# Loop one of a two-block network: where lower parts, weight copies and weight pieces stand in a step

## The chip, the core and the metric

The kernel runs on one core of a Trainium2 chip. The core has TensorE (PE in the profile; PEld is its weight loading), VectorE (DVE), ScalarE (ACT), GpSimd (POOL) and SyncE (SP), each with a queue of its own that is worked off in order, and 16 DMA engines. Matmuls read SBUF and write PSUM, which is used here as eight banks of 128 x 512 float32. The metric is the device time of one execution in microseconds (us), the median of several runs. Times inside an execution come from one profiled execution and are counted from the start of its span.

## What is computed

Two blocks over x of 32 batches, 128 rows, 512 columns, each steered by a condition of 512 numbers per batch. The first block's attention has 16 heads of 32 columns; loop one computes this block:

```python
h = _sln(hidden, w, ln_g, ln_b, Wg, bg, Wb, bb)
qkv = (h @ Wqkv.T + bqkv).reshape(B, N, num_heads, hd, 3)
...
energy = jnp.einsum('bhqd,bhkd->bhqk', q, k)
att = jax.nn.softmax(energy, axis=-1) / D ** 0.5
out = jnp.einsum('bhqk,bhkd->bhqd', att, v)
out = jnp.moveaxis(out, 1, 2).reshape(B, N, D)
out = out @ Wp.T + bp
h1 = out + hidden
h2 = _sln(h1, w, ln_g, ln_b, Wg, bg, Wb, bb)
return h2 + h1
```

`_sln` is a layer norm whose scale and shift come from the condition. The second block takes this result: an RMS norm with scale and shift, attention with one head of 512 columns, a projection, and an MLP of 512 to 2048 to 512 with an exact gelu, each with its residual. All tensors are float32.

## The kernel before

**Precision.** A float32 product is made from three products of reduced float32 parts: every operand is split into an upper part (a rounding copy, `h` at the end of a tile's name) and a lower part (operand minus upper part, `l`), and `mm3` sums upper x upper, lower x upper and upper x lower in one PSUM bank. So every operand costs a copy, mostly on ACT, and a subtraction on DVE or POOL before its matmuls can start.

**Tiling.** A batch is one tile of 128 x 512. Four batches make a group (G = 4) and 512 columns are four chunks of 128 (KC = 4). Eight groups times four chunks make the 32 steps of loop one (STEPS): step s belongs to group s // 4 and chunk s % 4, and handles in one go the four heads of this chunk for the four batches of the group. The rest of the program, about 545 us to the end, is block two, and is not touched by the change.

**One step.** The order of the calls in the loop's body is the order of each engine's queue; the compiler only adds semaphores and picks the buffers of a pool (the next free one of its kind). A step s issues, in this order:

- `energies(s+1)`: 16 matmuls of q and k into four banks (`pse`), four reduces on DVE (L577) to the negative maxima `nm`, a cast and a subtraction (L578, L579).
- `scores0(s)`: the energies again, transposed, on top of the spread maxima of the step before (`pst`, L602 and L606), in two banks of the kind `mm`, which `psv` and `psp` use too, and two of the kind `s`.
- `turned.low` (L461): the lower part of the normed batch whose upper part was made in the step before.
- `heads_out(s-1)`: attention times values (`pso`, L629) and the sums of the exponentials (`pss`, L634), in banks that `pse` used; their reciprocal by a logarithm and an exponential on ACT (L639, L640). `exponentials(s)` on ACT (L616).
- `past.first`, `past.sums`: the second layer norm's statistics of the batch that was finished in the step before.
- `divided0(s-1)`: three DVE instructions (L647 to L649) divide the heads' outputs; then ACT makes the upper part (`hi`, L651) and POOL the lower part (`lo`, L652). At the first step of a group it stands ahead of `end.bias` and `end.more`, otherwise behind them.
- `qk0(s+2)`: 12 matmuls for q (`psq`) and 12 for k (`psk`) of a coming step, from the normed batches of its group; ACT writes both with their bias (L548). Its second argument orders them by part instead of by chunk at the start of a group.
- between the two: `maxima(s+1)` (a transpose) and `spread_maxima(s+1)` (DVE, L590).
- `end.stream`: 12 matmuls (`psp`) for one batch of the group whose attention was done four steps ago, from `o`'s upper and lower parts; `end.bias` (POOL, L668) and `end.add` (DVE, L683) add bias, residual and product.
- `past.second` (L702), then `ready.merge` (DVE, L431: brings a batch that the DMA has transposed into the order of the matmuls) and `ready.rest` (ACT: four L448 with scale and shift, and the upper part, L457).
- `new.stats`, `end.add`, `new.norm`, and `past.third` (L711).
- work of single steps: `extras`, among them `weighted` in steps 0 and 1 (DVE, L505 and L507: four instructions whose result a matmul in the next step reads), and `split_w` in steps 0 to 3 (ACT L145, POOL L146).
- `values0`: 12 matmuls for v (`psv`), copied by ACT (L532).
- `new.halves`: ACT splits a normed batch into 16-bit halves (L422), and SP's queue starts its DMA transpose.
- from step 4 to 23, `weights.heads` and `weights.tails`: parts of the MLP's first weights are copied to upper parts by ACT (L920) and lower parts by POOL (L927), and SP's queue writes both out to DRAM (`put`). Per weight piece of five steps the numbers of copies are 2, 1, 1, 2, 1.

In the last three steps the loop also multiplies two weights of block two (`l1_vp`, `psvp`): four chunks `w1c2_0` to `w1c2_3` are loaded into buffers that q and k tiles use too, and each product is split by ACT (L126) and DVE (L127). `psvp0` takes a bank of the kind `s`. `vp_at` says that chunk 0 is requested in step 29, both 1 and 2 in step 30, and chunk 3 in step 31; the requests come a step ahead of the products.

Of the kernel before, what the change touches and what calls it, by code (L numbers as in the profile page):

```python
# [9 lines left out]
FP = mybir.dt.float32  # L10
# [3 lines left out]
ALU = mybir.AluOpType  # L14
# [4 lines left out]
KC = D // P  # L19
# [22 lines left out]
def cond_seq_kernel(ctx: ExitStack, tc, x, condT, wcond, w0, w1, wk1, wm1, wm2, cols, rows, out):  # L42
# [600 lines left out]
    def divided0(s):  # L643

        g, c = divmod(s, KC)
        pso, pss, w = es.pop(s)
        nc.vector.tensor_tensor(pss, pss, w, ALU.mult)  # L647
        nc.vector.tensor_tensor(w, pso, w, ALU.mult)
        nc.vector.scalar_tensor_tensor(w, pss, 2.0, w, ALU.subtract, ALU.mult, reverse0=True)  # L649
        hi, lo = (t[:, c] for t in os_[g])  # L650
        nc.scalar.copy(hi, w)  # L651
        nc.gpsimd.tensor_tensor(lo, w, hi.bitcast(FP), ALU.subtract)  # L652

    class End:

# [541 lines left out]
    with tc.manual_schedule(engines=ordered):  # L1197
# [88 lines left out]
        def l1_chunk(j, c):  # L1286
            return load(d_tile(f"w1c{j}_{c}", FP, (P, KC, P)), w1[:, j, :, ts(c, P)])
# [6 lines left out]
        def stage(work, get):  # L1294
            def begin():
                got = get()
                return lambda: work(got)

            return begin
# [10 lines left out]
            27: stage(l1_row, lambda: (weighted("wrow1", L1[3], C_BV1), row_of(R_BP1))),  # L1310
        }

        def vp_stage(c):
            return stage(lambda a: l1_vp(a, L1[3], c, s_tile if c == 0 else e_bank), lambda: l1_chunk(2, c))

        vp_at = {STEPS - 3: (0,), STEPS - 2: (1, 2), STEPS - 1: (3,)}
        FIRST1 = STEPS - G - 2

        def coming(s):
# [5 lines left out]
        CQ = range(7, 15, 2)  # L1325
        W_FIRST, W_STEPS = 4, len(Weights.TURNS)
        ready, new, end, past = new, coming(0), None, None
        staged = turned = None
        vps = []
        for s in range(STEPS):  # L1330
            last = s == STEPS - 1
            vps, vps_next = vps, [vp_stage(c) for c in vp_at.get(s + 1, ())]
            end = End(s - G, True, nc.scalar) if s >= G else None
            if not last:
                energies(s + 1)
            scores0(s)
            if turned:
                turned.low(nc.vector)
                turned = None
            if s:  # L1340
                heads_out(s - 1)
            exponentials(s)
            if past:
                past.first()
                past.sums()
            if s and s % KC == 0:
                divided0(s - 1)
            if end:
                end.bias()
                end.more()  # L1350
            if s % KC:
                divided0(s - 1)
            if staged:
                staged()
            if s > STEPS - 3:
                vps.pop(0)()
            vps_next = [begin() for begin in vps_next]
            q, k = qk0(s + 2, (s + 2) % KC == 0) if s + 2 < STEPS else ([], [])
            run(q)
            if not last:  # L1360
                maxima(s + 1)
                spread_maxima(s + 1)
            run(k)
            if end:
                run(end.stream())
            if s > STEPS - 3:
                end.add()
            if past:
                past.second()
            if ready and not last:  # L1370
                ready.merge()
                ready.rest()
            if new:
                new.stats()
            if end and s <= STEPS - 3:
                end.add()
            if new:
                new.norm()
            if s == KC + 1:
                cond_features()  # L1380
            if past:
                past.third()
            if "cq" in L1:
                L1.pop("cq")()
            if s < KC:
                split_w(W0["p"], raw["p"], s, nc.gpsimd)
            staged = extras[s + 1]() if s + 1 in extras else None
            if s <= B - G:
                run(values0(s - 1 + G))
            if vps:  # L1390
                vps.pop(0)()
            if new:
                new.halves()
            coming_new = None if last else coming(s + 1)
            q2, late = divmod(s - W_FIRST, 3)
            if not late and 0 <= q2 < 4:
                nc.scalar.dma_start(out=w2d[q2], in_=wm2[:, q2])
            wn, wj = divmod(s - W_FIRST, W_STEPS)
            if 0 <= wn < KC:
                weights.heads(wj)  # L1400
                weights.tails(wj)
            if not last:
                turned, ready, new = ready, new, coming_new
            vps = vps_next
            past = end
            if s in CQ:
                L1["cq"] = l1_cq(CQ.index(s))
            if s == 2:
                later["mods"] = r_tile("mods")
            wn, wj = divmod(s + 1 - W_FIRST, W_STEPS)  # L1410
            if 0 <= wn < KC and wj == 0:
                weights = Weights(wn)
            if s == STEPS - 2:
                l1_load()
        heads_out(STEPS - 1)
        past.first()
        past.sums()
        divided0(STEPS - 1)
        K = keys1(0)
        run(K[0])  # L1420

# [187 lines left out]
```

## Time and profile before

| | us |
|---|---|
| median of 3 runs (1446.51, 1448.55, 1450.84) | 1448.55 |
| the profiled execution's own time | 1445.18 |
| its span | 1443.0 |
| loop one within the span | 33.9 to 544.9 |
| TensorE busy | 1428.2 |
| VectorE busy | 1036.4 |
| ScalarE busy | 756.3 |
| GpSimd busy | 432.8 |
| mean granted TensorE clock | 0.999 |

The profiled execution is 2.2 us longer than its span and 3.4 us shorter than the median of the runs. In the span a group of lines of the profile reads: line and engine, what is written and read, how often, the time busy, the mean of one in nanoseconds, and the idle time of the engine ahead of it with the instruction that ended most of it. The chain of waits, followed back from the last instruction, goes along TensorE for 90% of the span:

```profile
PE 90%; DVE 6%; ACT 2%; DMA 2%; POOL 0%; issue 0%; SPq 0%; ACTq 0%; POOLq 0%; DVEq 0%
```

These are groups of the page that belong to loop one or reach into it:

```profile
L431 DVE COPY tn<-tn 128x1024 uint16<-128x1024 uint16 x90 | 103.9, 1155 | 5.3 <-DMA tn<-tn 5.3
...
L577 DVE TENSOR_REDUCE nm<-pse 128x4 f32<-128x512 f32 x128 | 79.5, 683 | 32.2 <-PE pse L565 31.9
...
L616 ACT ACTIVATE e<-pst 128x512 f32<-128x512 f32 x128 | 65.3, 595 | 1.3 <-PE pst L606 1.3
...
L448 ACT ACTIVATE tn<-tn,mod 128x128 f32<-128x128 f32 x104 | 42.9, 483 | 30.9 <-DVE tn L431 30.9
...
L927 POOL TENSOR_TENSOR wml<-wm,wmh 128x512 fp32r<-128x512 f32 x28 | 35.4, 1277 | 69.0 <-ACT wmh L920 64.8
...
L668 POOL TENSOR_TENSOR xe<-xe,row 128x512 f32<-128x512 f32 x32 | 44.9, 1403 | 6.7 <-DMA xe<-in_x 6.7
```

### The profile page before, as it was taken

How to read it: one execution, taken by the hardware profiler on the slowest of the kernel's cores; microseconds unless marked ns; L12 is line 12 of the kernel's file. 1: busy time of each engine (PE TensorE's matmuls, PEld its weight loads, DVE VectorE, ACT ScalarE, POOL GpSimd, SP SyncE). 2: the span in 40 equal slices, each digit the busy share in tenths (PEclk: the TensorE clock that was granted, in tenths of full speed). 3: DMA queues.
4: the chain of work that ended last, by engine and by line, in shares of the span. 5: the costliest groups of instructions: out<-in, count | busy, mean ns of one | idle time of the engine just before them, and what ended most of it. 6: DMA issues, size and time to landing. Idle time of an engine off the chain costs nothing.

```text
span 1443.0 us, 24819 instructions
## 1 busy us (share of the span) xinstructions
PE 1428.2 (99%) x9224; PEld 1146.3 (79%) x9224; DVE 1036.4 (72%) x1909; ACT 756.3 (52%) x1392; POOL 432.8 (30%) x393
## 2 busy tenths in 40 slices
PE   9999999999999999999999999999999999999998
PEld 5777777777777758888888888888888888888887
DVE  6778989898997878899987766655566556753442
ACT  4566565566664545677776444535453544523231
POOL 0124645555553334556550324000030002210000
PEclk9999999999999999999999999999999999999999
DMA  8267777967664555778888867747684777834450
GB/s 311 75 192 192 205 209 199 249 158 196 174 166 143 132 187 165 200 210 222 205 215 321 293 213 227 272 157 227 207 309 134 218 230 213 290 124 169 159 182 31
DMA packets 227873, 287.82 MB, mean 199 GB/s; under 512 B 107396, under 2 KB 138244, under 8 KB 226216
## 3 DMA queue, kind: packets, MB, share of 16 engines
q1 hardware_dynamic: 209888, 211.68, 50.0%
q10 hardware_dynamic: 17864, 74.55, 15.7%
q8 instruction: 73, 1.20, 0.3%
q14 instruction: 48, 0.39, 0.1%
HBM read 193.18 MB, written 73.60 MB: 185 GB/s over the span
## 4 chain that ended last, share of the span: by engine, by line
PE 90%; DVE 6%; ACT 2%; DMA 2%; POOL 0%; issue 0%; SPq 0%; ACTq 0%; POOLq 0%; DVEq 0%
PE acc L1053 24%; PE psh L164 21%; PE psp L164 6%; PE psq L164 5%; PE psV L164 5%; PE psT L164 5%; PE psk L164 5%; PE psv L164 5%; PE pse L565 2%; PE pso L629 2%; PE pss L818 2%; DVE nm L577 1%; PE pss L634 1%; PE pst L606 1%; PE pso L164 1%; PE psvp L757 1%
## 5 line engine op out<-in xcount | busy, mean ns | idle before, releaser
L337 POOL TENSOR_TENSOR rn<-vn,neghalf 128x1 f32<-128x1 f32 x96 | 58.1, 605 | 468.7 <-DVE vn L335 355.8
L422 ACT COPY tn<-x 128x1024 uint16<-128x1024 uint16 x90 | 94.1, 1047 | 52.4 <-DVE x L408 51.8
L991 ACT ACTIVATE c<-c,col 128x512 f32<-128x512 f32 x64 | 46.4, 725 | 141.9 <-DVE c L1016 88.8
L431 DVE COPY tn<-tn 128x1024 uint16<-128x1024 uint16 x90 | 103.9, 1155 | 5.3 <-DMA tn<-tn 5.3
L1069 POOL TENSOR_TENSOR xe<-xe,row 128x512 f32<-128x512 f32 x32 | 45.9, 1467 | 200.7 <-DVE u_7s L1045 116.4
L577 DVE TENSOR_REDUCE nm<-pse 128x4 f32<-128x512 f32 x128 | 79.5, 683 | 32.2 <-PE pse L565 31.9
L1006 DVE TENSOR_TENSOR c<-psh,ca 128x512 f32<-128x512 f32 x32 | 22.1, 692 | 87.5 <-PE psh L164 86.2
L616 ACT ACTIVATE e<-pst 128x512 f32<-128x512 f32 x128 | 65.3, 595 | 1.3 <-PE pst L606 1.3
L325 DVE BATCH_NORM_STATS2 stn<-x 128x6 f32<-128x512 f32 x96 | 65.2, 679 | 0.0
L408 DVE TENSOR_SCALAR x<-x,rn 128x512 f32<-128x512 f32 x64 | 58.3, 911 | 8.3 <-POOL rn L337 7.5
L337 POOL TENSOR_TENSOR re<-ve,neghalf 128x1 f32<-128x1 f32 x32 | 30.9, 965 | 105.6 <-DVE ve L330 102.0
L448 ACT ACTIVATE tn<-tn,mod 128x128 f32<-128x128 f32 x104 | 42.9, 483 | 30.9 <-DVE tn L431 30.9
L448 ACT ACTIVATE tn<-tn,mods 128x128 f32<-128x128 f32 x128 | 52.6, 484 | 11.7 <-DVE tn L431 11.7
L639 ACT ACTIVATE rs<-pss 128x512 f32<-128x512 f32 x32 | 19.1, 597 | 72.9 <-PE pss L634 72.9
L927 POOL TENSOR_TENSOR wml<-wm,wmh 128x512 fp32r<-128x512 f32 x28 | 35.4, 1277 | 69.0 <-ACT wmh L920 64.8
L1019 DVE TENSOR_TENSOR ca<-psh,ca 128x512 f32<-128x512 f32 x32 | 22.1, 691 | 41.8 <-PE psh L164 41.8
L668 POOL TENSOR_TENSOR xe<-xe,row 128x512 f32<-128x512 f32 x32 | 44.9, 1403 | 6.7 <-DMA xe<-in_x 6.7
L991 ACT ACTIVATE cb<-cb,col 128x512 f32<-128x512 f32 x32 | 23.2, 725 | 41.0 <-DVE cb L1020 41.0
L1073 DVE TENSOR_TENSOR xe<-acc,xe 128x512 f32<-128x512 f32 x32 | 21.1, 688 | 32.0 <-PE acc L1053 32.0
L565 PEld LDWEIGHTS pse<-qk 32*128 32x128 f32 x1024 | 32.1, 186 | 13.6 <-issue 5.3
L1003 ACT COPY ca<-psh 128x512 f32<-128x512 f32 x32 | 18.4, 575 | 43.0 <-PE psh L164 41.9
L565 PE MATMUL pse<-qk 32*128 32x128 f32 x1024 | 38.6, 283 | 1.5 <-ACT qk L548 1.4
(1387 smaller groups left out, 4702.7 us busy)
## 6 DMA issues: line engine op xcount, KB each, us to landing
mod<-mod SPq DMA_DIRECT2D x32, 512.0 KB, 4.6
ur<-ud SPq DMA_DIRECT2D x64, 256.0 KB, 4.4
xs<-xe SPq DMA_DIRECT2D x60, 256.0 KB, 2.8
xe<-xs SPq DMA_DIRECT2D x60, 256.0 KB, 3.0
x<-xs SPq DMA_DIRECT2D x59, 256.0 KB, 3.8
scw<-scw SPq DMA_DIRECT2D x32, 256.0 KB, 4.2
hTd<-tn SPq DMA_DIRECT2D x32, 256.0 KB, 6.6
hT<-hTd SPq DMA_DIRECT2D x32, 256.0 KB, 4.7
```

The costliest lines, as they stand in the source:

```text
L164: nc.tensor.matmul(st["ps"], *calls[j], start=(j == 0), stop=(j == n - 1))
L325: nc.vector.bn_stats(st, t)
L337: nc.gpsimd.tensor_tensor(r, v, neghalf, ALU.pow)
L408: nc.vector.tensor_scalar(X, X, r, None, ALU.mult)
L422: nc.scalar.copy(halves.rearrange("p (e d) -> p e d", e=2), X.bitcast(U16).rearrange("p (d e) -> p e d", e=2),)
L431: nc.vector.tensor_copy(self.a.bitcast(U16).rearrange("p (f e) -> p e f", e=2), self.t.bitcast(U16).rearrange("p (e f) -> p e f", e=2),)
L448: nc.scalar.activation(dst[:, c], self.a[:, ts(c, P)], AF.Identity, bias=m[:, q + B : q + B + 1], scale=m[:, q : q + 1],)
L565: nc.tensor.matmul(banks[r][:, ts(i, P)], q[32 * r : 32 * r + 32, ts(i, P)], k[32 * r : 32 * r + 32, ts(i, P)], start=True, stop=True,)
L577: nc.vector.tensor_reduce(nm[:, r], chunks(banks[r]), AX.X, ALU.max, negate=True)
L616: nc.scalar.activation(e, es[s][r], AF.Exp)
L991: nc.scalar.activation(t[nm], t[nm], AF.Gelu, bias=col[:, C_B1 + f : C_B1 + f + 1], scale=1.0)
L1053: nc.tensor.matmul(accs[i], u[pa][:, ts(i, P)], wb[f // 4][pb][:, f % 4, :], start=(first and j == 0), stop=(last and j == len(PARTS) - 1),)
```

## The change

Only the body of loop one and `divided0` change; the arithmetic stays as it is.

- The subtraction that makes the lower part of the heads' outputs leaves POOL (L652). A new function `lower0` issues it on DVE, behind `spread_maxima` and ahead of `past.second`. The upper copy on ACT stays in `divided0`.
- A batch's lower part (L461) is issued at the end of the step that makes its upper part, behind `past.third`, and no longer in the next step behind the reduces. It stands ahead of the `weighted` instructions of the step's extras.
- `weights.heads` and `weights.tails` move from the end of a step to a place ahead of `past.third`, and so ahead of the copy of v and of `new.halves` with its transpose.
- `divided0` stands behind `end.bias` and `end.more` in every step, and `qk0` orders its 12 matmuls by chunk in every step.
- The chunks for `l1_vp` are requested one at a time: chunk 0 in step 29 behind the k matmuls, chunk 1 at the end of step 29, chunk 2 in step 30 ahead of `past.first`, chunk 3 in step 30 behind the k matmuls. The products keep their places: 0 at the end of step 29, 1 in the middle and 2 at the end of step 30, 3 in the middle of step 31.

```diff
@@ -647,9 +647,14 @@
         nc.vector.tensor_tensor(pss, pss, w, ALU.mult)
         nc.vector.tensor_tensor(w, pso, w, ALU.mult)
         nc.vector.scalar_tensor_tensor(w, pss, 2.0, w, ALU.subtract, ALU.mult, reverse0=True)
+        nc.scalar.copy(os_[g][0][:, c], w)
+        es[s] = w
+
+    def lower0(s):
+
+        g, c = divmod(s, KC)
         hi, lo = (t[:, c] for t in os_[g])
-        nc.scalar.copy(hi, w)
-        nc.gpsimd.tensor_tensor(lo, w, hi.bitcast(FP), ALU.subtract)
+        nc.vector.tensor_tensor(lo, es.pop(s), hi.bitcast(FP), ALU.subtract)
 
     class End:
 
@@ -1310,10 +1315,14 @@
             27: stage(l1_row, lambda: (weighted("wrow1", L1[3], C_BV1), row_of(R_BP1))),
         }
 
-        def vp_stage(c):
-            return stage(lambda a: l1_vp(a, L1[3], c, s_tile if c == 0 else e_bank), lambda: l1_chunk(2, c))
-
-        vp_at = {STEPS - 3: (0,), STEPS - 2: (1, 2), STEPS - 1: (3,)}
+        chunk = {}
+
+        def vp_load(c):
+            chunk[c] = l1_chunk(2, c)
+
+        def vp(c):
+            l1_vp(chunk.pop(c), L1[3], c, e_bank if c else s_tile)
+
         FIRST1 = STEPS - G - 2
 
         def coming(s):
@@ -1325,42 +1334,40 @@
         CQ = range(7, 15, 2)
         W_FIRST, W_STEPS = 4, len(Weights.TURNS)
         ready, new, end, past = new, coming(0), None, None
-        staged = turned = None
-        vps = []
+        staged = None
         for s in range(STEPS):
             last = s == STEPS - 1
-            vps, vps_next = vps, [vp_stage(c) for c in vp_at.get(s + 1, ())]
             end = End(s - G, True, nc.scalar) if s >= G else None
             if not last:
                 energies(s + 1)
             scores0(s)
-            if turned:
-                turned.low(nc.vector)
-                turned = None
             if s:
                 heads_out(s - 1)
             exponentials(s)
+            if s == STEPS - 2:
+                vp_load(2)
             if past:
                 past.first()
                 past.sums()
-            if s and s % KC == 0:
-                divided0(s - 1)
             if end:
                 end.bias()
                 end.more()
-            if s % KC:
+            if s:
                 divided0(s - 1)
             if staged:
                 staged()
             if s > STEPS - 3:
-                vps.pop(0)()
-            vps_next = [begin() for begin in vps_next]
-            q, k = qk0(s + 2, (s + 2) % KC == 0) if s + 2 < STEPS else ([], [])
+                vp(1 if s == STEPS - 2 else 3)
+            q, k = qk0(s + 2) if s + 2 < STEPS else ([], [])
             run(q)
             if not last:
                 maxima(s + 1)
                 spread_maxima(s + 1)
+            if s:
+                lower0(s - 1)
             run(k)
+            if s > STEPS - 4 and not last:
+                vp_load(0 if s == STEPS - 3 else 3)
             if end:
                 run(end.stream())
             if s > STEPS - 3:
@@ -1378,8 +1385,14 @@
                 new.norm()
             if s == KC + 1:
                 cond_features()
+            wn, wj = divmod(s - W_FIRST, W_STEPS)
+            if 0 <= wn < KC:
+                weights.heads(wj)
+                weights.tails(wj)
             if past:
                 past.third()
+            if ready and not last:
+                ready.low(nc.vector)
             if "cq" in L1:
                 L1.pop("cq")()
             if s < KC:
@@ -1387,21 +1400,18 @@
             staged = extras[s + 1]() if s + 1 in extras else None
             if s <= B - G:
                 run(values0(s - 1 + G))
-            if vps:
-                vps.pop(0)()
+            if STEPS - 4 < s < STEPS - 1:
+                vp(0 if s == STEPS - 3 else 2)
             if new:
                 new.halves()
+            if s == STEPS - 3:
+                vp_load(1)
             coming_new = None if last else coming(s + 1)
             q2, late = divmod(s - W_FIRST, 3)
             if not late and 0 <= q2 < 4:
                 nc.scalar.dma_start(out=w2d[q2], in_=wm2[:, q2])
-            wn, wj = divmod(s - W_FIRST, W_STEPS)
-            if 0 <= wn < KC:
-                weights.heads(wj)
-                weights.tails(wj)
             if not last:
-                turned, ready, new = ready, new, coming_new
-            vps = vps_next
+                ready, new = new, coming_new
             past = end
             if s in CQ:
                 L1["cq"] = l1_cq(CQ.index(s))
@@ -1416,6 +1426,7 @@
         past.first()
         past.sums()
         divided0(STEPS - 1)
+        lower0(STEPS - 1)
         K = keys1(0)
         run(K[0])
 
```

## The prediction

> **What bounds the kernel now.** I read the page's busy shares and chain first, then the list of waits, then the starts of TensorE's groups step by step, and last the timelines around each irregular step.
>
> ```profile
> PE 1428.2 (99%) x9224; PEld 1146.3 (79%) x9224; DVE 1036.4 (72%) x1909; ACT 756.3 (52%) x1392; POOL 432.8 (30%) x393
> ```
>
> (the page's busy line) TensorE works in 99% of the span, so only three things can move the time: its idle gaps, its pipeline's short stalls, which count as busy, and its clock. The gaps add up to 9.5 us after the first instruction, and all but 0.18 lie before 519 us, in the preamble and loop one. The code behind loop one keeps its order and its engines.
>
> The waits that TensorE has in the loop (engine, line, releaser: total, times, longest):
>
> ```profile
> PE pst L602 <- DVE w1vpl L127: 1.9, 1, 1.9
> PE pso L629 <- DVE nm L577: 1.8, 4, 0.7
> PE psq L164 <- DVE n_24l L461: 1.4, 1, 1.4
> PE pse L565 <- ACT qk L548: 1.4, 1, 1.4
> PE psp L164 <- POOL o2l L652: 0.4, 1, 0.4
> ```
>
> I number a step by the energies (pse) that open its segment: segment i holds energies(i), issued by step i-1 of the loop. Undisturbed segments (i = 8, 12, 14, 17, 18, 20 to 22 and others) last 15.34 to 15.35 us; T below is the start of pse. The losses against that sit in a few:
>
> - Lower parts late at a group's boundary. psq takes 2.86 us; in segments 7, 11, 19 and 23 it takes 3.39, 3.63, 3.47 and 4.58 (+0.53, 0.77, 0.61, 1.72). psp takes 2.72, in segment 13 3.43 (+0.71). Sum 4.34.
> - The tail, segments 30 and 31, lines below.
> - v copies on ACT that end after T+0.85: pst 0.2 to 0.5 late in segments 9, 15, 16, 19, 25 (1.3 together); and 0.4 each in 2 to 5.
> - Reduces (L577) late for pso in 3, 7, 10 and 28: 0.74, 0.39, 0.55, 0.40.
>
> ```profile
> 392.11 1.77 DVE L461 TENSOR_TENSOR n_24l<-tn,n_24h 128x512 fp32r<-128x512 f32 x1
> ...
> 513.99 0.69 ACT L548 ACTIVATE qk<-psq,col 128x512 f32<-128x512 f32 x1 [7.06 <-PE psvp L757]
> ...
> 517.94 0.69 DVE L127 TENSOR_TENSOR w1vpl<-psvp,w1vph 128x512 fp32r<-128x512 f32 x1 [5.39 <-ACT w1vph L126]
> ```
>
> (timelines: start, duration, instruction, idle before and releaser) The first is the lower part that psq waited for until 393.94. The second is ACT held 7.06 us: the last qk tile takes the buffer of the weight chunk that psvp was still reading. That makes pse 1.36 us late at 515.30, and the copies of the same ACT queue late, so that L127 frees a score bank at 518.6 and pst starts 1.89 us late. What it sets off shows in the windows (stretch, length, PE, PEld, DVE, ACT and POOL busy, granted clock, DMA):
>
> ```profile
> 515.71:519.13 3.42, 1.53 (x45) 1.22 (x42) 1.19 (x2) 3.12 (x6) 0.00 (x0) 1.00 0.37 96
> 519.13:522.55 3.42, 3.42 (x66) 3.06 (x62) 3.35 (x8) 0.00 (x0) 0.00 (x0) 0.50 0.75 182
> ```
>
> The granted clock was 0.50 for 3.41 us after a stretch with TensorE busy 0.45 of it; that costs half of 3.41, 1.7 us. A gap of 1.43 (at 392.5) and the one of 1.36 (at 513.9) were followed by a clock of 1.00; busy shares there were 0.58 and 0.60.
>
> **Gains.** *Boundaries.* L461 now runs at the end of its batch's own step, half a step or more ahead of its matmuls, and o's lower part (32 x 1.30 to 1.74 us on POOL) is one DVE subtraction right behind spread_maxima. All 4.34 us of waits have one of the two as releaser: **-4.3** (-3.6 to -4.4, the bound being one boundary of 0.7 that persists).
>
> *Tail.* Chunks asked for one at a time no longer put a chunk into qk31's buffer, so 1.36 + 1.89 + 1.7 = 4.95 can go. psvp's 20 matmuls a piece stay. The bank that psvp0 takes still comes free only behind an ACT copy and L127 (0.58 + 0.69), about T+1.3 against pst at T+0.9, so some 0.2 to 1.0 stays: **-4.8** (-3.9 to -5.0).
>
> **What is hidden.** DVE gains 32 subtractions. L461's clean row is 0.68 us, its contended one 1.77, and the new one has the same operands. In segment 17 DVE is busy 14.16 of 15.60 us. The contended instructions there are part of that:
>
> ```profile
> 304.46 1.68 POOL L652 TENSOR_TENSOR o3l<-rs,o3h 128x512 fp32r<-128x512 f32 x1 [1.12 <-ACT o3h L651]
> 306.09 1.78 POOL L668 TENSOR_TENSOR xe<-xe,row 128x512 f32<-128x512 f32 x1
> ...
> 304.90 1.85 DVE L431 COPY tn<-tn 128x1024 uint16<-128x1024 uint16 x1
> ```
>
> The merge takes 1.85 beside POOL and about 0.75 where POOL is still. With L652 gone, L668 can start where POOL came free, at 303.3, and end near 305; the merge starts 0.7 later than now, at 305.6 (behind the subtraction), so they part and it ends some 0.3 earlier (0 to 0.4). DVE's sum changes by +0.7 to 1.4 less up to 1.1: 14.2 to 15.2 of 15.34. I cost this at 0 on the path; the cover is the wait of 1.16 us that the reduces have for pse at the step's start. Gone, each 0.1 us beyond it would cost 0.1 in each of 26 steps. Late reduces in 7 and 10 lose L461 ahead but gain it behind: **0** (-0.9 to +0.5). divided0's fixed place and qk0's order (the same 12 matmuls) are 0 too: L590 stands behind both as before.
>
> **Losses.** *First steps.* Steps 0 and 1 end with `weighted` on DVE, whose rows now stand behind L461, and L461 behind ACT's upper copy (L457):
>
> ```profile
> 59.99 0.62 ACT L457 CAST n_4h<-tn 128x512 fp32r<-128x512 f32 x1
> ...
> 58.51 0.48 DVE L505 TENSOR_SCALAR wwu<-w1r,col 128x512 f32<-128x512 f32 x1
> 59.02 2.33 DVE L507 SCALAR_TENSOR_TENSOR wwu<-w1r,col,wwu 128x512 f32<-128x512 f32 x3
> 61.54 2.49 DVE L577 TENSOR_REDUCE nm<-pse 128x4 f32<-128x512 f32 x4 [0.19 <-PE pse L565]
> ```
>
> Before, `weighted` ran at 58.51 to 61.35 while ACT was busy. Now L461 starts at 60.61, ends 61.29, `weighted` ends at 64.13 (65.0 if L507 meets POOL's 1.3 us L146), and the reduces start there instead of 61.54. pso comes one reduce (0.73) later: 64.86 to 65.75 instead of 62.98, so +1.9 to 2.8. In segment 3 L457 ends at 74.52, `weighted` at 78.0 to 78.9 instead of 76.9: +1.1 to 2.0. In segments 4 and 5 no `weighted` stands there. **+3.9** (3.0 to 4.8).
>
> *Clock.* The first of these idles falls into a stretch that would be busy 0.36 to 0.45; the row above dropped at 0.45 and 0.58 did not. Two chances of 1.7 us at about 60% each: **+2.0** (0 to 3.4).
>
> [...]
>
> *Weight heads ahead of the v copy.* In steps 4 to 23 one or two ACT copies (L920, 0.52 us from start to start) and their puts move ahead of the v copy; on POOL L927 moves with them, on SP the puts move ahead of the transpose that the next merge waits for. ACT waits for psv before the v copy by 1.2 us or more in segments 8, 11, 12, 20, 21, 24, and by 0.3 to 0.8 in 6, 10, 13, 14, 17, 18, 22, 23: a single copy hides there. It doesn't in 9, 16 and 19 (two copies, L457 ending at T+0.62, 0.83, 0.62) nor in 15 and 25:
>
> ```profile
> 168.60 0.62 ACT L457 CAST n_12h<-tn 128x512 fp32r<-128x512 f32 x1
> 169.12 0.58 ACT L532 COPY v<-psv 128x512 f32<-128x512 f32 x1
> ...
> 170.55 0.62 ACT L920 CAST wmh<-wm 128x512 fp32r<-128x512 f32 x1
> ```
>
> A v copy then ends at T+2.2 for two copies where T+0.85 is free: +1.1 in each of 9, 16, 19, +0.5 in 15 and 25, +0.5 in 6 and 14: 5.3 if the merge comes no earlier, and 2.5 if it comes 0.3 to 0.4 earlier. If the merge comes a whole 1.1 earlier, the present lateness goes too: -0.6. A put whose transpose is late (landing 2.8 to 4.6 us is usual for 256 KB on SP, up to 10.8 in four steps beside the 1 MB w2d copies) is in the upper end. **+2.5** (-0.6 to 5.6).
>
> **Sum.** -4.3 - 4.8 + 0 + 3.9 + 2.0 + 2.5 = **-0.7 us** on the profiled execution's 1445.18, 1444.5. That execution lies 3.4 below the median of the runs shown, 1448.55; a median after is then 1447.8.
>
> **Rivals.**
>
> *The losses stay hidden (faster).* L461's input could come early enough in steps 0 and 1, or the gate stay open, and the earlier merge absorb the heads. For it: in segments 8, 11, 12 and 20 ACT idles 1.2 us ahead of the v copy. Against: L457's times in segments 2 and 3 follow from TensorE's order, not from DVE. With 1 us of losses left: -9.1 + 1 = -8.1, 1440.5.
>
> *DVE's in-order end of step (slower).* At the end of every step DVE has, in order, the last L711, then L461, then the reduces that pso waits for. L711 ended at 309.65 in segment 17, T+0.02 of the next. If L461 meets POOL's moved L927 it lasts 1.77, ends at T+1.8, and the reduces start 0.6 later than the T+1.2 of now; 0.35 of that is slack. The point from which it decides is L461 ending at T+1.55. At 0.3 in each of some 20 steps: +6, sum +5.3, 1453.9. Against: the earlier merge moves L711 forward in most steps, and the heads come ahead of L461, so that L927 may be done.
>
> *The tail's gain doesn't come (slower or nothing).* psvp1 and psvp2 stand in step 30 as before, and chunk 2 waits on SP for psvp0's reads. If that chunk lands late, psvp2 waits as much as is removed: +4.1, 1452.7. Against: 256 KB land in 3 to 5 us, and a third of a step lies between.
>
> **Chances.** 0.3% is 4.35 us, about what a measurement of this kernel tells from no change. The sum's case 0.50 (own range 1442.5 to 1452: faster 0.12, same 0.34, slower 0.04), hidden losses 0.24 (0.23 faster), DVE's end of step 0.20 (0.17 slower), the tail 0.06 (half slower). Faster 0.35, same 0.41, slower 0.24. The range from 1440.3 to 1454 takes in the middles of the cases on both sides.
>
> **What will show it.** psq at 2.86 in segments 7, 11, 19, 23 and no L461 or L652 releaser among TensorE's waits; no ACT wait of 7 us near 507, clock 1.00 at 519 to 523; pso late by about 2 us in segment 2 and above 1 in segment 3 with a DVE releaser, and a granted clock of 0.50 behind; pst above 1.5 in segments 9, 16, 19; the merge near 0.8 us. The forecast is wrong if DVE's reduces start later than T+1.6 in ordinary segments, or if segments 2 and 3 keep their 13.9 and 14.6 us.

## The result and the profile after

The changed kernel takes 1454.99 us, the median of 12 runs (1451.06 to 1461.76), against 1448.26 (12 runs, 1445.41 to 1450.84) for the kernel before on the same chip. The ratio is 1.0053, with a 95% interval of 1.0037 to 1.0069: 6.7 us slower, where 0.7 us less was forecast, and outside the range of 1440.3 to 1454.

The profiled execution took 1451.06 us with a span of 1449.3, 6.2 longer than the span before. The page's busy lines and the chain of waits:

```profile
PE 1427.4 (98%) x9224; PEld 1145.4 (79%) x9224; DVE 1033.5 (71%) x1941; ACT 757.5 (52%) x1392; POOL 388.8 (27%) x361
...
PE 85%; DVE 7%; DMA 4%; ACT 2%; issue 1%; POOL 0%; ACTq 0%; SPq 0%; DVEq 0%; POOLq 0%
```

TensorE does the same work in the same time, but the chain leaves it for 15% of the span instead of 10. POOL lost 44 us to DVE, and DVE is none the busier, although it has 32 instructions more. The waits of TensorE (engine, line, releaser: total, times, longest):

```profile
PE pso L629 <- DVE nm L577: 11.9, 12, 2.7
PE pst L602 <- ACT v L532: 2.8, 4, 1.0
```

(From L657 on, the subtraction in `lower0`, the changed kernel's lines are five higher: its L688, L716, L770, L925, L932 and L935 are L683, L711, L765, L920, L927 and L930 of the kernel before.) All waits for a lower part (L461, L652), for the last qk tile and for w1vpl are gone, as the change has it. In their place the reduces are late, 12 times instead of 4, and 11.9 us instead of 1.8. The lengths of the segments, from one start of pse to the next (segment 31 to the first psT), in the two profiled executions; those left out agree within 0.06 us:

| segment | before | after | difference |
|---|---|---|---|
| 2, 3 | 13.90, 14.61 | 16.73, 16.72 | +4.94 |
| 10, 16 | 15.89, 15.80 | 19.43, 17.31 | +5.05 |
| 12, 14 | 15.35, 15.35 | 16.35, 17.46 | +3.11 |
| 18, 24 | 15.35, 15.35 | 15.77, 15.81 | +0.89 |
| 9, 11, 13, 15, 19, 23, 25 | 15.59, 16.11, 16.07, 15.54, 16.20, 17.07, 15.53 | 15.35, 15.74, 15.35, 15.35, 15.77, 15.80, 15.35 | -3.41 |
| 30, 31 | 17.49, 29.55 | 16.06, 26.03 | -4.95 |
| behind loop one | 898.18 | 899.16 | +0.97 |

With 0.34 less ahead of the loop that is the 6.2 us. (Half of the 0.97 is a longer wait of psaT for DVE's L852; it was not followed up.) The gains came, and the three places below cost more than they brought.

**Segments 2 and 3.** The timeline of DVE around the start of segment 2 (start, duration, engine, instruction, idle before and its releaser; T is 60.02):

```profile
60.31 0.69 DVE L461 TENSOR_TENSOR n_4l<-tn,n_4h 128x512 fp32r<-128x512 f32 x1 [2.05 <-ACT n_4h L457]
60.92 1.52 DVE L505 TENSOR_SCALAR wwu<-w1r,col 128x512 f32<-128x512 f32 x1
62.48 2.33 DVE L507 SCALAR_TENSOR_TENSOR wwu<-w1r,col,wwu 128x512 f32<-128x512 f32 x3
64.72 2.48 DVE L577 TENSOR_REDUCE nm<-pse 128x4 f32<-128x512 f32 x4
```

DVE stands 2.05 us in front of L461 with the weighted instructions ready behind it; the reduces start at T+4.7 instead of T+1.2. TensorE is idle for 2.73 us ahead of pso here, and for 2.74 in segment 3.

**Segments 12 and 14** (the timeline of the changed kernel; segment 14 starts at 255.41):

```profile
253.93 1.78 DVE L716 SCALAR_TENSOR_TENSOR scw<-xe,scw 128x512 f32<-128x512 f32 x1
...
255.64 1.76 DVE L461 TENSOR_TENSOR n_16l<-tn,n_16h 128x512 fp32r<-128x512 f32 x1
257.32 1.75 DVE L770 SCALAR_TENSOR_TENSOR wk<-wk,row 128x512 f32<-128x512 f32 x1
...
259.00 1.87 DVE L577 TENSOR_REDUCE nm<-pse 128x4 f32<-128x512 f32 x3
...
253.60 3.25 POOL L932 TENSOR_TENSOR wml<-wm,wmh 128x512 fp32r<-128x512 f32 x2 [1.34 <-ACT wmh L925]
256.82 1.71 POOL L935 TENSOR_TENSOR wm<-wm 128x512 f32<-128x512 f32 x1
```

Three DVE instructions of 0.68 us take 1.75 to 1.78 each while POOL works on the weights' lower parts, which the moved heads release just there. L770 is the product with the bias that `l1_cq` leaves in L1 and steps 8, 10, 12 and 14 take; it stands behind L461 and ahead of the reduces, which start at T+3.6. Between 100 and 545 us, 22 instructions of these three kinds (L716, L461, L770) last over 1.2 us, and every one lies beside L932 or L935; before the change there were 4.

**Segments 10 and 16.** Here the merge waits for its transpose, as it does ahead of segment 7. Rows of the changed kernel (an SP row's duration is read as the time its queue is held: the 5.89 us of the transpose end at 182.72, and SP's next row starts at 182.81; segment 10 starts at 188.55, segment 16 at 288.22):

```profile
175.63 1.11 SPq L939 DMA_DIRECT2D ad<-wml  x1
176.83 5.89 SPq L426 DMA_TRANSPOSE tn<-tn  x1
...
186.68 0.75 DVE L431 COPY tn<-tn 128x1024 uint16<-128x1024 uint16 x1 [3.59 <-DMA tn<-tn]
...
274.95 5.86 SPq L426 DMA_TRANSPOSE tn<-tn  x1
...
288.92 1.13 ACT L925 CAST wmh<-wm 128x512 fp32r<-128x512 f32 x2
289.96 0.57 ACT L532 COPY v<-psv 128x512 f32<-128x512 f32 x1
...
289.99 1.76 DVE L770 SCALAR_TENSOR_TENSOR wk<-wk,row 128x512 f32<-128x512 f32 x1
```

The same transpose, merge and v copy of segment 16 in the kernel before, where it starts at 278.49:

```profile
264.97 2.16 SPq L426 DMA_TRANSPOSE tn<-tn  x1
...
275.79 1.19 DVE L431 COPY tn<-tn 128x1024 uint16<-128x1024 uint16 x1 [3.15 <-DMA tn<-tn]
...
279.22 0.58 ACT L532 COPY v<-psv 128x512 f32<-128x512 f32 x1
```

These late transposes stand right behind one of the four 1 MB copies to `w2d` that ACT's queue starts in steps 4, 7, 10 and 13, and the merge waited for them before the change too: 1.62, 0.50 and 3.15 us ahead of segments 7, 10 and 16, now 3.17, 3.59 and 3.15. Ahead of segment 16 the transpose starts 2.1 us into its segment (2.0 before), so it is not what the change made worse; new there is what stands behind the merge: two weight copies put the end of the v copy at T+2.3 instead of T+1.3, and L770 takes 1.76 instead of 0.69. In segment 10 TensorE waits 0.88 us for the v copy and 0.97 for the reduces, and 1.7 of the 3.5 us are the clock (an estimate: half of the 3.41 us in which it was granted at 0.50, from 193.24 on; last section).

### The profile page after: what moved, and what is told of

Read it like the earlier page. It is cut to its first block, busy times and chain, and to the rows that moved or that the text cites. A ratio compares the mean times of both kernels' runs of the same rounds, so it can differ in the third digit from the quotient of the medians.

```text
span 1449.3 us, 24799 instructions
## 1 busy us (share of the span) xinstructions
PE 1427.4 (98%) x9224; PEld 1145.4 (79%) x9224; DVE 1033.5 (71%) x1941; ACT 757.5 (52%) x1392; POOL 388.8 (27%) x361
## 4 chain that ended last, share of the span: by engine, by line
PE 85%; DVE 7%; DMA 4%; ACT 2%; issue 1%; POOL 0%; ACTq 0%; SPq 0%; DVEq 0%; POOLq 0%
PE acc L1058 24%; PE psh L164 21%; PE psV L164 5%; PE psT L164 5%; PE psq L164 5%; PE psp L164 5%; PE psk L164 5%; PE psv L164 3%; PE pso L629 2%; PE pss L823 2%; PE pss L634 2%; PE pso L164 1%; DMA xe<-in_x 1%; PE pse L565 1%; PE psvp L762 1%
## 5 line engine op out<-in xcount | busy, mean ns | idle before, releaser
L1074 POOL TENSOR_TENSOR xe<-xe,row 128x512 f32<-128x512 f32 x32 | 45.0, 1434 | 203.3 <-DMA xe<-xs 177.4
L431 DVE COPY tn<-tn 128x1024 uint16<-128x1024 uint16 x90 | 80.4, 893 | 13.4 <-DMA tn<-tn 13.4
L932 POOL TENSOR_TENSOR wml<-wm,wmh 128x512 fp32r<-128x512 f32 x28 | 43.3, 1557 | 27.5 <-ACT wmh L925 26.1
L629 PE MATMUL pso<-e,v 128*32 128x128 f32 x1024 | 35.4, 280 | 11.9 <-DVE nm L577 11.9
L673 POOL TENSOR_TENSOR xe<-xe,row 128x512 f32<-128x512 f32 x32 | 42.3, 1321 | 18.1 <-DMA xe<-in_x 12.5
L532 ACT COPY v<-psv 128x512 f32<-128x512 f32 x32 | 18.7, 584 | 41.0 <-PE psv L164 40.8
```

What stands on the lines that cost most here:

```text
L431: nc.vector.tensor_copy(self.a.bitcast(U16).rearrange("p (f e) -> p e f", e=2), self.t.bitcast(U16).rearrange("p (e f) -> p e f", e=2),)
L629: nc.tensor.matmul(pso[rr, ts(i, P)], v[:, i, 32 * (4 * c + r) : 32 * (4 * c + r) + 32], e[r][:, ts(i, P)], start=True, stop=True,)
```

## The experiments

Each is the changed kernel with the edit shown, unless it says otherwise. "Before" beside each is the kernel before, run on the same chip.

**1. Heads and tails back at the end of the step.**

```diff
-            wn, wj = divmod(s - W_FIRST, W_STEPS)
-            if 0 <= wn < KC:
-                weights.heads(wj)
-                weights.tails(wj)
             if past:
                 past.third()
...
                 nc.scalar.dma_start(out=w2d[q2], in_=wm2[:, q2])
+            wn, wj = divmod(s - W_FIRST, W_STEPS)
+            if 0 <= wn < KC:
+                weights.heads(wj)
+                weights.tails(wj)
```

> The change with the weight heads and tails put back behind the halves, at the end of the step; nothing else differs. Theory A (the end of the step on DVE: in the four steps with the bias product L770 it comes behind the lower part L461, and both run beside POOL's moved L932, 1.76 us each instead of 0.68): the contention goes, segments 12 and 14 fall back to about 15.4 to 15.8 and segments 10 and 16 keep what their late transposes cost; segments 2 and 3 stay at 16.7. Time 4 to 6 us below the changed kernel, 1449 to 1451 against 1455. Rival B (the extra subtraction makes DVE the bound): no change, 1454 to 1456. Rival C (the heads ahead of the v copy and the puts ahead of the transpose on SP make merges and v copies late): segments 7, 10, 12, 14 and 16 all go back to the times before, 8 us less, about 1447.

Measured: 1441.13 (before 1447.80; ratio 0.995, 0.9938 to 0.9962), 13.9 below the changed kernel. Segments 7, 12, 14, 16, 18, 19, 23 and 24 are all at 15.35, 10 at 15.77; 2 and 3 stay at 16.69 and 16.71. Segment 14 in this kernel starts at 250.25:

```profile
249.37 0.69 DVE L461 TENSOR_TENSOR n_16l<-tn,n_16h 128x512 fp32r<-128x512 f32 x1
249.97 0.68 DVE L770 SCALAR_TENSOR_TENSOR wk<-wk,row 128x512 f32<-128x512 f32 x1
...
251.44 2.48 DVE L577 TENSOR_REDUCE nm<-pse 128x4 f32<-128x512 f32 x4 [0.78 <-PE pse L565]
253.96 1.07 DVE L578 CAST nmx<-nm 128x16 fp32r<-128x16 f32 x1
...
252.48 2.51 POOL L932 TENSOR_TENSOR wml<-wm,wmh 128x512 fp32r<-128x512 f32 x2 [4.48 <-ACT wmh L925]
```

The same instructions, 0.69 and 0.68; DVE waits for pse again, and L932 lies beside the reduces, which keep their 2.48, and beside L578, which takes 1.07 instead of 0.17 and holds nothing up. TensorE's waits, and the transpose ahead of segment 10:

```profile
PE pso L629 <- DVE nm L577: 6.1, 4, 2.7
...
PE pst L602 <- ACT v L532: 0.3, 1, 0.3
...
174.76 1.54 SPq L426 DMA_TRANSPOSE tn<-tn  x1
```

Of the 11.6 us that this span is shorter than the changed kernel's, 5.8 are waits for the reduces, 2.5 waits for v copies, and 1.7 the clock's drop in segment 10, which is not there. So the heads' move costs all that segments 7 to 24 lost and more, and the extra DVE subtractions cost nothing there while POOL is quiet. The gain was larger than any theory had: the copies, puts and POOL work moved together, and the next runs try to part them.

**2. The lower part behind the weighted and bias products of its step.**

```diff
-            if ready and not last:
-                ready.low(nc.vector)
             if "cq" in L1:
...
             staged = extras[s + 1]() if s + 1 in extras else None
+            if ready and not last:
+                ready.low(nc.vector)
```

> The change with the lower part L461 issued behind the bias product and the weighted instructions of its step instead of ahead of them. Theory A: in segments 2 and 3 the weighted instructions no longer wait for ACT's upper copy; segment 2 comes to about 14.0 to 14.4 (16.73 now), segment 3 to 14.8 to 15.5 (16.72 now); segments 10 to 16 keep their time, since the sum on DVE ahead of the reduces is the same. 3.5 to 4.9 us below the changed kernel, 1450 to 1451.5. Rivals B and C: less than 1 us of change, 1454 to 1456.

Measured: 1448.49 (before 1447.80; ratio 1.0005, 0.9996 to 1.0013), 6.5 less. Segment 3 is 15.18, as theory A had it, and segment 2 14.61, 0.2 above its range: DVE's in-order wait is their price. These two give 3.7 us; part of the rest goes with the clock, whose mean was 0.997 to 1.000 in these runs and 0.993 to 0.999 in those of the changed kernel.

**3. The bias product ahead of L688.**

```diff
-            if "cq" in L1:
-                L1.pop("cq")()
...
+            if "cq" in L1:
+                L1.pop("cq")()
             if end and s <= STEPS - 3:
                 end.add()
```

> The change with the bias product L770 (steps 8, 10, 12, 14) issued ahead of the addition L688, where DVE waits for psp, instead of behind L461. Theory A: the reduces of segments 10, 12, 14 and 16 start 1.7 us earlier; 12 falls to 15.35, 14 from 17.46 to 15.7, 10 and 16 by 1 to 1.7 each. 5 to 6.5 us below the changed kernel, 1448.5 to 1450. Rival B: L770 costs DVE the same wherever it stands, no change. Rival C: the merges are late as before, less than 2 us gained, 1453 to 1455.

Measured: 1451.94 (before 1447.80; ratio 1.0024, 1.0015 to 1.0034), 3.1 less, between the theories. Segment 14 comes to 15.77 as expected, 12 to 15.74, 0.4 above, and 10 to 17.18; but 16 takes 20.36: a granted clock of 0.50 from 293.34 to 296.75 makes 1.7 us of that, and with the merge late pst waits 0.87 us for L688, which now stands behind L770. L770 is most of the price of 12 and 14; 10 and 16 have another.

**4. The heads' lower part back on POOL,** with divided0 in its new place.

```diff
-            if s:
-                lower0(s - 1)
...
-        nc.scalar.copy(os_[g][0][:, c], w)
-        es[s] = w
+        hi, lo = (t[:, c] for t in os_[g])
+        nc.scalar.copy(hi, w)
+        nc.gpsimd.tensor_tensor(lo, w, hi.bitcast(FP), ALU.subtract)
```

> The change with the lower part of the heads' outputs back on POOL in divided0 (behind end.bias in every step). Theory A: DVE loses 0.69 us a step, but the merge runs beside POOL again, 1.7 instead of 0.75, so the end of the step on DVE is no earlier; segments 2 and 3 stay, 10 to 16 stay or get worse by up to 1 each, boundaries lose up to 1 again; 1455 to 1459. Rival B: DVE's load is what costs; the time falls to 1448 or below. Rival C: no change, 1454 to 1456.

Measured: 1453.10 (before 1447.80; ratio 1.0039, 1.0027 to 1.0052). Rival B's 1448 is refuted; theory A's 1455 was too high by 2. The segments say more: 11, 18, 19, 23 and 24 fall to 15.35 and 14 to 16.29, while 9 rises to 17.90, with a wait of psp for L652 of 2.3 us. Segment 14 starts at 259.35 here:

```profile
257.80 0.68 DVE L711 SCALAR_TENSOR_TENSOR scw<-xe,scw 128x512 f32<-128x512 f32 x1
...
258.41 1.76 DVE L461 TENSOR_TENSOR n_16l<-tn,n_16h 128x512 fp32r<-128x512 f32 x1
...
257.96 3.35 POOL L927 TENSOR_TENSOR wml<-wm,wmh 128x512 fp32r<-128x512 f32 x2 [1.34 <-ACT wmh L920]
```

With the merge at 1.83 beside POOL again, ACT's copies and so POOL's L927 come at T-1.4, behind most of L711, which takes 0.68; in the changed kernel the merge takes 0.74, L932 comes at T-1.8 and meets L716 as well. The quick merge, a gain by itself, thus adds to the price of the moved heads.

**5. Tails back at the end of the step, heads early.**

```diff
-                weights.tails(wj)
...
                 nc.scalar.dma_start(out=w2d[q2], in_=wm2[:, q2])
+            if 0 <= wn < KC:
+                weights.tails(wj)
```

> The change with only the weight tails (POOL's L932 and the puts of the lower parts) back at the end of the step; the ACT copies and the puts of the upper parts stay ahead of the v copy and the transpose. Theory A1 (what the early heads and tails cost is POOL's L932 beside the last DVE instructions of the step): nearly all of the early heads' price goes, segments 12, 14, 18, 19, 23 and 24 at 15.35 to 15.5, 10 and 16 within 1 us of 15.5; 1442 to 1446. Theory A2 (SP: the puts ahead of the transposes make the merges late): segments 10 and 16 stay above 16.3 and 12 and 14 fall only where they follow; 1448 to 1452. Theory A3 (ACT: the copies ahead of the v copy): unchanged, 1453 to 1456.

Measured: 1450.76 (before 1446.21; ratio 1.0027, 1.0016 to 1.0037). Segments 10 and 16 are at 16.87 and 17.72, 12 and 14 at 16.35 and 16.37, as A2 has it, but A1 was not put to the test: POOL has nothing else to do and starts L932 as soon as the early copies are there (in segment 10 at 192.63, and ACT's L925 ends at 192.55), so the contention stayed (L770 takes 1.77 at 193.00). Here POOL's start is set by the input, not by the place in its queue.

**6. Copies early, all puts called behind the halves.** `put` only keeps its arguments, and a new `puts` issues the DMAs.

```diff
                 nc.scalar.dma_start(out=w2d[q2], in_=wm2[:, q2])
+            if 0 <= wn < KC:
+                weights.puts()
```

> The change with the upper and lower copies where it puts them, but all their DMA puts issued at the old place, behind the transpose on SP. Theory A1: segments 12 and 14 stay at 16.3 and 17.4, 18, 19, 23 and 24 at 15.8, only 10 and 16 gain; 1451 to 1455. Theory A2: the merges wait for no transpose any more, segments 7, 10 and 16 come to 15.8 or below, and 12 and 14 with them if their DVE work was late for that reason; 1444 to 1449. Theory A3: unchanged.

Measured: 1454.37 (before 1446.21; ratio 1.0055, 1.004 to 1.007), as the changed kernel. SP's rows in segment 10:

```profile
192.57 0.37 SPq L948 DMA_DIRECT2D ad<-wmh  x1
194.25 0.37 SPq L948 DMA_DIRECT2D ad<-wml  x1
...
195.37 1.42 SPq L426 DMA_TRANSPOSE tn<-tn  x1
```

The puts stand ahead of the transpose as in the changed kernel, though they are called behind it; number 5 shows the same for the lower part (194.77, the transpose 195.25). So, other than said of one step above, the order of the calls is not the order of SP's queue; what sets it was not looked into. The run says nothing of theory A2, which stays without an experiment of its own.

**7. Number 1, with the lower parts of steps 0 and 1 behind the next step's reduces.**

```diff
-            if ready and not last:
+            if ready and not last and s > 1:
                 ready.low(nc.vector)
...
             scores0(s)
+            if turned:
+                turned.low(nc.vector)
...
+                turned = ready if s < 2 else None
```

> The change with heads and tails back at the end of the step, and the lower part L461 of steps 0 and 1 alone issued behind the next step's reduces, as before the change. If the price of the first steps is the in-order wait of the weighted instructions and of the reduces for L461, segments 2 and 3 come back to 13.9 and 14.6, and the time is 4.9 below that of the kernel with only the heads put back, plus what the clock gate took there in some runs: 1434.5 to 1437. If their price has another cause, 1441 as that kernel.

Measured: 1434.45 (before 1446.21; ratio 0.9919, 0.9906 to 0.9932). Segments 2 and 3 are 13.91 and 14.59, those of before. Their price is settled.

**8. The kernel before with the weight pieces alone** asked for one at a time; the other hunks are those of the change that name `vp`.

```diff
-        vp_at = {STEPS - 3: (0,), STEPS - 2: (1, 2), STEPS - 1: (3,)}
+        def vp_load(c):
+            chunk[c] = l1_chunk(2, c)
+
+        def vp(c):
+            l1_vp(chunk.pop(c), L1[3], c, e_bank if c else s_tile)
```

> The kernel before with only the weight pieces asked for one at a time. If the tail's gain belongs to this part alone, segments 30 and 31 lose 4.95 and nothing else moves: 1442.5 to 1444 against 1447.8. If it needs the other parts (an ACT queue that is shorter for other reasons), less than 2 us.

Measured: 1440.79 (before 1446.21; ratio 0.9958, 0.9946 to 0.997), 5.4 less. Segments 30 and 31 lose 1.42 and 3.52; the tail's gain belongs to this part alone.

**9. Heads early, tails in the next step behind end.bias,** so that POOL is quiet at a step's end.

```diff
-                weights.tails(wj)
+                tail = lambda w=weights, j=wj: w.tails(j)
...
                 end.bias()
                 end.more()
+            if tail:
+                tail()
+                tail = None
```

> The change with the weight tails (POOL's L932, their sums and the puts of the lower parts) issued in the next step behind POOL's end.bias, so that POOL is quiet at the end of a step; the ACT copies and the puts of the upper parts stay where the change has them. The run with the tails at the end of the step did not part the two, since POOL started L932 as soon as the copies were there. Theory A1 (POOL beside the last DVE instructions): segments 12 and 14 at 15.35 to 15.5, 18, 19, 23 and 24 at 15.35; 10 and 16 below 16.3; 1443 to 1446 with the first steps' price still in. Theory A2 or A3 (puts of the upper parts ahead of the transposes, copies ahead of the v copy): 10 and 16 stay above 16.8, 12 and 14 fall less; 1448 to 1452.

Measured: 1451.46 (before 1447.46; ratio 1.0029, 1.0017 to 1.0042). Mixed: segment 12 is at 15.35 and 14 at 16.17, with L461 and L770 clean (0.69, 0.68), as A1 has it; 10 and 16 stay at 19.64 (1.7 of it the clock) and 16.93, as A2 and A3 have it. And the contention has moved on:

```profile
248.50 1.77 DVE L707 SCALAR_TENSOR_TENSOR xe<-te,re,xe 128x512 f32<-128x512 f32 x1
250.19 1.84 DVE L431 COPY tn<-tn 128x1024 uint16<-128x1024 uint16 x1
...
249.68 3.47 POOL L935 TENSOR_TENSOR wm<-wm 128x512 f32<-128x512 f32 x2
```

Now L707 and the merge run at 1.8, L457 ends at T+0.16, and the two head copies push the v copy's end to T+1.68 in segment 14: pst is late there.

**10. Number 7 with split_w of steps 0 to 3 behind the halves.**

```diff
-            if s < KC:
-                split_w(W0["p"], raw["p"], s, nc.gpsimd)
...
                 new.halves()
+            if s < KC:
+                split_w(W0["p"], raw["p"], s, nc.gpsimd)
```

> The kernel of the first-steps run with split_w of steps 0 to 3 issued behind the halves, so that ACT's L145 no longer stands ahead of the v copy. If the 0.4 us that pst is late in segments 2 to 5 comes from that, segments 2 to 5 lose 0.4 each: 1432.5 to 1433.5 against 1434.5. If not, 1434.5.

Measured: 1432.72 (before 1447.46; ratio 0.9896, 0.9882 to 0.991). Segments 2, 4 and 5 lose 0.4 each, segment 3 1.1 against the kernel before. This is the fastest version of the study, 1.0% below the kernel before.

**11. Number 1 with every lower part behind the next step's reduces.**

```diff
-            if ready and not last:
-                ready.low(nc.vector)
...
             scores0(s)
+            if turned:
+                turned.low(nc.vector)
+                turned = None
```

> The change with heads and tails back at the end of the step and every lower part L461 behind the next step's reduces, as before the change; left of the change are the heads' lower part on DVE, the places of divided0 and qk0 and the weight pieces. Theory: the boundary waits of psq come back, 3 to 5 us more than with L461 at its own step's end: 1437.5 to 1439.5 against 1434.5. Rival (the boundary waits came from POOL beside L461, and go with the heads' lower part leaving POOL): 1434.5 to 1436.

Measured: 1445.55 (before 1447.46; ratio 0.9987, 0.9978 to 0.9996), 11 above number 7, or 9.8 by the two ratios, since the kernel before took 1446.21 beside number 7; the theory had 3 to 5. The waits of TensorE:

```profile
PE psq L164 <- DVE n_24l L461: 2.1, 1, 2.1
PE psq L164 <- DVE n_20l L461: 2.1, 1, 2.1
...
PE psq L164 <- DVE n_8l L461: 1.2, 1, 1.2
PE psq L164 <- DVE n_12l L461: 1.2, 1, 1.2
```

With qk0 ordered by chunk the second matmul reads a lower part, where the order by part had four upper ones first; so the boundaries cost more than in the kernel before. With qk0 in this order, L461 at its own step's end is worth all of that.

**12. Number 7 with the heads' lower part on POOL.** The edit is that of number 4.

> The kernel of the first-steps run with the lower part of the heads' outputs back on POOL. Theory: the psp wait at one boundary (0.7) and the v copies behind a merge that runs beside POOL (1.3 in all) come back, 1 to 3 us more than 1434.5: 1435.5 to 1437.5. Rival B (the subtraction on DVE costs): 1433.5 or less.

Measured: 1438.74 (before 1447.46; ratio 0.994, 0.9927 to 0.9952), 4.3 above number 7, or 3.0 by the two ratios. In the span only 0.4 of 4.1 us lie ahead of block two (segment 9 takes 0.5 more, and a psp wait of 0.2 for L652 is back); 3.7 lie in block two, where an idle gap of 1.93 us stands ahead of psaT at 778 and a clock of 0.50 follows. So the waits that the theory named hardly came back. Why psaT is late there was not followed up; the runs' mean clocks of 0.998 and 0.999, against 1.000 in number 7, fit a drop in each.

## Why the prediction was wrong

*Boundaries (-4.3).* Right: psq takes 2.86 to 2.90 in 7, 11, 19 and 23, and psp 2.72 in 13. Late reduces took back 0.4 in 11, 19 and 23, and a late v copy 1.0 in 7.

*Tail (-4.8).* Right: -4.95, shown by number 8. What remains of the late score bank is a gap of 0.07 and a slow pst.

*First steps (+3.9).* Right in mechanism and a little short: +4.94, where 3.0 to 4.8 stood. L505 met POOL's L146 in both segments and took 1.52 instead of 0.48.

*Clock (+2.0).* The term went to the wrong place. In the profiled execution the two idles of 2.7 us were followed by no drop, and segment 10 by one of 1.7 us. In other runs the first steps had it (number 5: 18.35 and 18.31 in segments 2 and 3, and a granted clock of 0.50 from 67.13 to 70.54, in segment 2). The runs of the changed kernel have mean granted clocks of 0.993 to 0.999, the one of 1451.06 us 0.999 and the one of 1460.78 us 0.993; number 7, without such idles, has 1.000 in all. Part of the 3.9 us between the profiled execution and the median goes with it: a mean clock that is lower by 0.001 is 1.45 us of this span (an estimate from its length). What lowers the clock, for which the first rival and number 7's expectation have a name, no trace shows; the traces show its granted value, 1.00 or 0.50.

*Weight heads ahead of the v copy (+2.5).* This step failed. Putting heads and tails back gains 11.6 in the span and 13.9 in the median (number 1); the term's range ended at 5.6. What it reckoned, late v copies, came to 2.5 us of waits, and that this is its figure is luck: the copies in 9 and 19 were not late at all, since the merge now takes 0.75 and ends earlier; they were in 7, 10 and 16, where the merge waits for its transpose. What it left out of the sum is POOL: L932, which the early copies release, lies beside the last DVE instructions of the step, and TensorE waits 5.8 us more for the reduces; a drop of the clock adds 1.7.

*"I cost this at 0 on the path; the cover is the wait of 1.16 us that the reduces have for pse at the step's start."* This holds with POOL quiet (number 1) and failed beside the moved heads. The sum over a step was even too high: DVE is busy 13.11 us in segment 17, 13.90 before, where 14.2 to 15.2 stood (its own terms give 13.8 to 15.6). But the end of the step was not costed instruction by instruction: L770 was left out, though it stands behind L461 in four steps, and L461, L716 and L770 were taken as clean. The rival "DVE's in-order end of step" named L461 beside L927 and a price of 0.3 in each of 20 steps; it came as 3.1 us in segments 12 and 14, where L770 adds to it, and about 0.4 in 11, 18, 19, 23 and 24. Against it stood that the earlier merge would bring relief; it brought L932 forward too (number 4). That the rival's 1453.9 lies near the 1454.99 is in part luck, since the upper end of the first steps, segments 10 and 16 and the clock are in it.

*The puts.* The transpose that the merge ahead of segment 10 needs was issued at 174.76 in number 1, 1.7 us into its segment, and held SP for 1.54; with the puts ahead it was issued at 176.83, 3.6 into its segment, and held SP for 5.89, and the merge waited 3.59. That the puts are the cause in segment 10 is read from these rows; no run isolates it, and a 1 MB copy runs beside the transpose in both. (Between 90 and 400 us the transposes without such a copy land 3.1 to 5.4 us after their issue in the kernel before and 3.1 to 8.3 in the changed one.)

## What to carry to other kernels

Where two engines slow each other down (here DVE's 0.68 us became 1.75 to 1.78 beside POOL, and POOL's two L932 took 3.25 there and 2.51 in number 1), a moved instruction is costed by what runs beside it in its new place, and also by whom its result sets going: an early copy on ACT sent POOL into the three DVE instructions that TensorE waits for next. An engine's busy time over a step says little when the end of the step has a deadline; list what stands in its queue between the last free input and the deadline, in the irregular steps too. And a bundle of moves is worth taking apart: by the ratios of numbers 8, 11, 7 and 1 to the kernel before, added in this order, the weight pieces are worth -0.42%, the heads' lower part with the new places of divided0 and qk0 +0.29, L461 at its own step's end -0.68, the same in the first two steps +0.31, and the weight heads +1.03; together the +0.53 of the change. Each is good to about 0.2 either way, an estimate from the intervals, and they hold in this order only: the +0.29 has in it the late L461 behind qk0 ordered by chunk, which the next part then takes away.

## What was not expected of the hardware

In these traces the busy share of a stretch did not decide alone whether the clock dropped. The stretches of the changed kernel (stretch, length, busy times and counts, granted clock, DMA) are counted from the clock's first record at 5.51 in steps of 3.413 us, the length of its record at 0.50 (ahead of that one stand 187.73 us at 1.00, 55 such steps):

```profile
63.55:66.96 3.41, 1.50 (x40) 1.03 (x40) 3.37 (x6) 0.00 (x0) 0.00 (x0) 1.00 0.38 72
66.96:70.38 3.42, 3.42 (x18) 2.19 (x13) 2.14 (x6) 2.88 (x6) 0.00 (x0) 1.00 0.23 77
...
189.84:193.25 3.41, 1.56 (x40) 1.26 (x41) 3.41 (x7) 1.88 (x3) 1.60 (x1) 1.00 0.75 213
193.25:196.66 3.41, 3.41 (x40) 1.80 (x40) 2.95 (x8) 0.00 (x0) 0.24 (x1) 0.50 1.11 262
```

A stretch busy for 1.50 us was followed by 1.00, one busy for 1.56 by 0.50. The first holds pso and pss, the second nearly all pst, whose matmuls read 32 partitions (32x128 and 32x512 in the profile); that the kind of matmul counts is a guess that no run tried, and the partitions alone don't explain it: in number 12 a stretch busy for 1.48 us (775.36 to 778.77), with psh and psaT on 128 partitions, was followed by 0.50 too. The drop of the changed kernel came after gaps of 0.88 and 0.97 us in one stretch, and gaps of 2.73 and 2.74 us were followed by none.
